# Two tiles instead of three for gathered embedding rows, and the gathers of a time step issued behind the transposes of the step two before it

## The chip, the cores and the metric

The kernel runs on one core of one Trainium2 chip. The metric is the device time of one execution in microseconds. Before the change the median of three runs is 1648.53 us (1646.59 to 1648.6).

## The reference

A batch of 1024 sequences, each of 50 item numbers, is looked up in an embedding table of 100001 rows of 128 numbers. Row 0 counts as zero.

```
emb    = emb_table.at[0].set(0.0)
e      = emb[seq]                                  # 1024 x 50 x 128
prefix = cumsum(e, axis=1)
uF     = prefix / minimum(t_idx, lengths)          # running mean
y      = (uF - mean) * rsqrt(var + 1e-5) * gamma + beta   # mean, var over the batch, per step
step:    v = v + (x - v) / 2; spike = v >= 1; v = v - spike     # 50 steps, one after the other
scores = spikes.mean(axis=0) @ emb.T               # 1024 x 100001
```

The output alone is 409.6 MB. The 50 steps depend on one another through the prefix sum and through v.

## The kernel before, in words

The kernel has two stages. The first works through the 50 time steps and makes the spike counts, a 128 x 1024 tile (embedding dimension on partitions, batch along the free dimension). The second multiplies the counts by the table, 1024 rows of it at a time, and stores the scores; it is bound by those stores and is not touched by the change.

A time step t of the first stage (the loop at L296) goes like this.

- POOL gathers: gather(t) (L192) takes a tile "e" of the pool "gather" (L170) and issues eight indirect DMAs (L195), called lanes here, each of 128 rows of 512 bytes. The tile is 128 x 1024 numbers.
- PE: eight transposes of the gathered tile (L308), four for each half of the batch, accumulate onto the prefix sum in the two PSUM banks "pre". Two further matmuls, correct(t+1) (L268), one for each half, prepare the next step: they take off the rows that items with number 0 have put in. They are issued after the transposes of step t but each waits for DVE to have read its half of "pre".
- DVE: for each half, L317 makes the running mean uF out of "pre", and L318 its statistics. Then come L322, a few small operations, the resting potential (L284), the spike count (L287) and the new v (L345). Every fifth step, only() (L258) makes the weights of the next five corrections.
- ACT: the square root (L326), the centring of uF (L327), the scaling into v (L342), and the comparison with the threshold (L280).

In steps 42 and 44, prepare() transposes and splits a first block of the table for the second stage (L358 to L370; its eight transposes are at L123).

The order of each engine's instructions is the order in which the program issues them (a manual schedule); waits are put between engines where a tile is written, read or used again. A pool with bufs=n hands out n tiles in turn: a new tile of the same tag waits until the last use of the tile n before it has ended. So with three tiles, lane 0 of gather(t+2), issued at the head of step t (L299), waits for the last transposes of step t-1. On POOL's queue there is nothing else during the loop; all later gathers stand behind a lane that waits. Each lane also waits for the same lane of the gather before to have landed (eight completion semaphores, used in turn), and each transpose waits for the landing of its own lane.

Ahead of the loop two tiles of the same pool serve the setup: isz (a 0/1 mask of the items with number 0) and rb (the reciprocal lengths), L203 and L204; each is transposed by PE (L212, L231) and then free. gather(0) is issued behind their allocation, gather(1) just ahead of the loop (L295). The uF tiles come from another pool with two tiles (L169), of the same size. After the loop one output tile of the second stage's first products is taken from the pool "gather" as well (L397).

Of the kernel before, what the change touches and what calls it, by code (L numbers as in the profile page):

```python
# [12 lines left out]
F32 = mybir.dt.float32  # L13
# [7 lines left out]
P = 128  # L21
# [15 lines left out]
def rec_kernel(  # L37
# [10 lines left out]
    B, T = seq.shape  # L48
    N, D = table.shape
    NB = B // P  # L50
# [30 lines left out]
    def pair(i):  # L81
        free.append([embp.tile([P, HALF], F32R, tag=f"{x}{i}", name=f"{x}_{i}") for x in ("hi", "lo")])
# [54 lines left out]
    def prepare(q, pt):  # L137
        turned(q, pt)
        split[q] = hi, lo = free.pop(0)
        hw = size(q)  # L140
        if hw % 2:
            nc.vector.memset(hi[:, hw : hw + 1].bitcast(F32), 0.0)
            nc.vector.memset(lo[:, hw : hw + 1].bitcast(F32), 0.0)
        vp, vh, vl = views(q, pt, hi, lo)
        nc.scalar.copy(vh, vp)  # L145
        nc.vector.tensor_tensor(vl, vp, vh.bitcast(F32), ALU.subtract)  # L146
# [18 lines left out]
    with ExitStack() as ph:  # L165
# [1 line left out]
        lp = ph.enter_context(tc.tile_pool(name="lif", bufs=1))  # L167
        sp = ph.enter_context(tc.tile_pool(name="stats", bufs=3))
        up = ph.enter_context(tc.tile_pool(name="uF", bufs=2))  # L169
        gp = ph.enter_context(tc.tile_pool(name="gather", bufs=3))  # L170
        accp = ph.enter_context(tc.tile_pool(name="acc", bufs=1, space=bass.MemoryType.PSUM))
        vp = ph.enter_context(tc.tile_pool(name="v", bufs=1, space=bass.MemoryType.PSUM))

# [18 lines left out]
        def gather(t):  # L192
            es[t] = gp.tile([P, B], F32, tag="e", name=f"e_{t}")
            for n in range(NB):
                nc.gpsimd.indirect_dma_start(  # L195
                    out=es[t][:, n * P : (n + 1) * P],
                    out_offset=None,
                    in_=table,
                    in_offset=bass.IndirectOffsetOnAxis(ap=idx[:, n, t : t + 1].bitcast(U32), axis=0),
                )  # L200

        make_identity(nc, ident)
        isz = gp.tile([P, NB, P], F32, tag="e", name="isz")  # L203
        rb = gp.tile([P, NB, P], F32, tag="e", name="rb")  # L204
        gather(0)

        nc.vector.memset(isz, 0.0)
# [45 lines left out]
        def only(t):  # L253

            k = t % ONLY
            if k == 0:
                n = min(ONLY, T - t)
                nc.vector.tensor_tensor(  # L258
                    ls[:, :n, :],
                    r0n.unsqueeze(1).to_broadcast([P, n, D]),  # L260
                    sel[:, t : t + n].unsqueeze(2).to_broadcast([P, n, D]),
                    ALU.mult,
                )
            return ls[:, k, :]

        def correct(t, l):
            for h in range(B // BANK):
                nc.tensor.matmul(  # L268
                    pre[h],
                    lhsT=l,  # L270
                    rhs=zT[:, h * BANK : (h + 1) * BANK],
                    start=t == 0,
                    stop=False,
                    skip_group_check=True,
                )

        def over(t, v):

            d = lp.tile([P, B], BF16, tag="d", name=f"d_{t}")
            nc.scalar.activation(d, v, AF.Identity, bias=less)  # L280
            return d

        def rest(d, v):
            nc.vector.scalar_tensor_tensor(negv, d, 0.0, v, ALU.is_ge, ALU.subtract)  # L284

        def spiked(out, cs, v):
            nc.vector.scalar_tensor_tensor(out, v, V_TH, count[:, cs], ALU.is_ge, ALU.add)  # L287
# [7 lines left out]
        gather(1)  # L295
        for t in range(T):  # L296
            last = t == T - 1
            if t + 2 < T:
                gather(t + 2)  # L299
            e = es.pop(t)  # L300
            if last:
                rest(d, v)
                spiked(count, whole, v)
            uF = up.tile([P, B], F32, tag="uF", name=f"uF_{t}")
            bs = sp.tile([P, B // BANK, 6], F32, tag="bs", name=f"bs_{t}")
            for h, cs in enumerate(halves):
                for k in range(0, BANK, P):
                    nc.tensor.matmul(  # L308
                        pre[h][:, k : k + P],
                        lhsT=e[:, h * BANK + k : h * BANK + k + P],  # L310
                        rhs=ident,
                        start=False,
                        stop=last,
                        is_transpose=True,
                        skip_group_check=True,
                    )
                nc.vector.scalar_tensor_tensor(uF[:, cs], rlen[:, cs], 1.0 / (t + 1), pre[h], ALU.max, ALU.mult)  # L317
                nc.vector.bn_stats(bs[:, h, :], uF[:, cs])  # L318
            if not last:
                correct(t + 1, l)  # L320
            mv = sp.tile([P, 2], F32, tag="mv", name=f"mv_{t}")
            nc.vector.bn_aggr(mv, bs.rearrange("p h s -> p (h s)"))  # L322


            r = sp.tile([P, 1], F32, tag="r", name=f"r_{t}")
            nc.scalar.activation(r, mv[:, 1:2], AF.Sqrt, bias=eps)  # L326
            nc.scalar.activation(uF, uF, AF.Identity, bias=mv[:, 0:1], scale=-1.0)  # L327


            if t and not last:  # L330
                rest(d, v)

            nc.vector.reciprocal(r, r)
            q = sp.tile([P, 1], F32, tag="q", name=f"q_{t}")
            nc.vector.scalar_tensor_tensor(q, mv[:, 1:2], BN_EPS, r, ALU.add, ALU.mult)
            nc.vector.tensor_scalar(q, q, r, 3.0, ALU.mult, ALU.subtract)
            a = sp.tile([P, 1], F32, tag="a", name=f"a_{t}")
            nc.vector.tensor_scalar(a, q, r, hgb[:, 0:1], ALU.mult, ALU.mult)  # L338


            def x(vt, cs):
                nc.scalar.activation(vt, uF[:, cs], AF.Identity, bias=hgb[:, 1:2], scale=a)  # L342

            def step(vt, cs):
                nc.vector.scalar_tensor_tensor(vt, negv[:, cs], -0.5, vt, ALU.mult, ALU.add)  # L345

            if not last:
                vt = vp.tile([P, B], F32, tag=f"v{t % 2}", name=f"v_{t}")
                x(vt, whole)
                if t:  # L350
                    spiked(count, whole, v)
                step(vt, whole)
                v = vt
                d = over(t, v)
                if t + 2 < T:
                    l = only(t + 2)

                if t in (T - 8, T - 6):  # L358
                    q = (t - T + 8) // 2
                    pair(q)  # L360
                    prepare(q, vp.tile([P, HALF], F32, tag="v1", name=f"pt_{q}"))
                    if q == TWICE - 1:
                        for k in range(TWICE):
                            rows[GROUP + k] = first[:, k, :]
                        nc.sync.dma_start(
                            out=first[:, :TWICE, :],
                            in_=table[GROUP * HALF : (GROUP + TWICE) * HALF, :].rearrange(
                                "(q p k) d -> p q (k d)", p=P, k=KQ
                            ),
                        )  # L370
# [54 lines left out]
    for c, W in enumerate(WIDTHS):  # L425
# [30 lines left out]
        for n in range(NB):  # L456
            if c == 0 and n == 0:
                continue
            pool, tag, most = turns[blocks % len(turns)]
# [51 lines left out]
```

## Time and profile before

| | |
|---|---|
| median of three runs | 1648.53 us |
| the profiled execution, its own time | 1649.66 us |
| its span in the profile | 1647.8 us |
| mean granted PE clock | 0.791 |
| busy over the span: PE, DVE, ACT, POOL | 65%, 57%, 41%, 23% |
| first stage, 0 to 580 us: PE, DVE, ACT, POOL busy | 177.1, 361.2, 184.8, 381.4 us |
| first stage: granted PE clock, DMA share | 0.52, 0.26 |
| second stage, 580 to 1647.8 us: PE, DVE, ACT, POOL busy | 892.6, 582.8, 484.4, 0.0 us |
| second stage: granted PE clock, DMA share | 0.94, 0.98 |

The page of the profile cuts the span into 40 slices and prints the busy share of each engine in tenths; lists the costliest groups of instructions by line, with count, total and mean time, and the idle time ahead of them with what ended most of it; and follows the chain of work that ended last. Other views list waits by engine and line, instructions in order of time, and busy times by stretch. In a timeline each line has the start in us, the duration, the engine, the line of the program, the operation, output and inputs, and in brackets the idle time of the engine ahead of it and what ended it. A releaser called "remote" or "issue" is one that the profile could not name. An instruction on POOL that issues an indirect DMA is recorded as busy while the descriptors are made; the transfer comes after.

In the text a gather, a step or a transpose is counted from 0 by its order in the trace, which is the order of the program: gather(t) is the eight lanes of step t.

### The profile page before, as it was taken

The page shows a single profiled execution, that of the slowest core. Times are in us where ns is not written, and L with a number is a line of the kernel's source. Part 1 is how long each engine was busy: PE and PEld are TensorE (multiplying, and loading weights), DVE is VectorE, ACT ScalarE, POOL GpSimd, SP SyncE. Part 2 cuts the span into 40 slices and gives each one's busy share as a digit, 9 for nine tenths or more (in the row PEclk, how much of TensorE's full clock was granted, in tenths as well). Part 3 has the DMA queues.
Part 4 walks back from the last instruction along what each step waited for, and adds up shares of the span by engine and source line. Part 5 has one row for each costly group of instructions (what it writes and reads, how often), then busy time and mean ns, then how long its engine had stood idle before and what let it go on. Part 6 is the DMA issues. An engine that isn't in the chain of part 4 may idle for free.

```text
span 1647.8 us, 12231 instructions
## 1 busy us (share of the span) xinstructions
PE 1069.7 (65%) x4450; PEld 816.8 (50%) x4450; DVE 944.0 (57%) x1122; ACT 669.2 (41%) x697; POOL 381.4 (23%) x406
## 2 busy tenths in 40 slices
PE   4233332222322488888988888888887888888884
PEld 2022221111211376666866666666666666666763
DVE  5366665656665866556755455555555555555552
ACT  2133332323322455455644444444444444444442
POOL 7676666666666500000000000000000000000000
PEclk7555555555555589999999999989999999999998
DMA  9511111111111269999999999999999999999998
GB/s 345 209 50 46 46 47 46 45 46 49 46 45 46 64 285 416 405 421 418 399 425 429 430 429 423 416 434 418 427 427 416 416 421 417 428 427 423 396 431 342
DMA packets 53689, 488.12 MB, mean 296 GB/s; under 512 B 11995, under 2 KB 12796, under 8 KB 32380
## 3 DMA queue, kind: packets, MB, share of 16 engines
q1 hardware_dynamic: 32256, 429.81, 62.0%
q0 software_dynamic: 12800, 26.24, 5.9%
q10 hardware_dynamic: 8572, 31.28, 4.8%
q8 instruction: 35, 0.57, 0.1%
q14 instruction: 26, 0.21, 0.0%
HBM read 77.69 MB, written 409.60 MB: 296 GB/s over the span
## 4 chain that ended last, share of the span: by engine, by line
DMA 45%; DVE 20%; PE 11%; another core or an unknown queue 10%; ACT 7%; issue 4%; POOL 1%; ACTq 0%; SPq 0%; DVEq 0%
DMA scores<-o 45%; PE po L153 10%; ACT o L471 5%; DVE bs L318 4%; DVE uF L317 3%; DVE v L345 3%; DVE negv L284 3%; DVE count L287 2%; ACT v L342 2%; DVE o L469 1%; POOL e L195 1%; PE pre L268 1%; DVE a L338 1%; DVE mv L322 1%
## 5 line engine op out<-in xcount | busy, mean ns | idle before, releaser
L469 DVE TENSOR_SCALAR o<-po 128x1024 f32<-128x1024 f32 x391 | 464.4, 1221 | 344.7 <-DMA scores<-o 310.4
L471 ACT ACTIVATE o<-po 128x1024 f32<-128x1024 f32 (+1 forms) x391 | 389.7, 1018 | 538.8 <-DMA scores<-o 324.6
L195 POOL DMA_INDIRECT e<-in_L_rec_emb_table,idx x400 | 380.7, 952 | 184.6 <-issue 114.9
L153 PE MATMUL po<-pairs,countB 128*128 128x512 f32 x1136 | 305.1, 414 | 59.8 <-ACT o L471 42.8
L268 PE MATMUL pre<-zT,ls 128*128 128x512 f32 x100 | 78.7, 789 | 364.1 <-DVE uF L317 267.1
L153 PEld LDWEIGHTS po<-pairs,countB 128*128 128x128 f32 x1136 | 218.0, 197 | 122.9 <-ACT o L471 57.9
L153 PE MATMUL po<-pairs,countC 128*128 128x512 f32 x852 | 236.4, 424 | 44.8 <-ACT o L471 44.8
L268 PEld LDWEIGHTS pre<-zT,ls 128*128 128x128 f32 x100 | 28.8, 289 | 407.7 <-DVE uF L317 297.2
L153 PEld LDWEIGHTS po<-pairs,countC 128*128 128x128 f32 x852 | 167.0, 203 | 90.7 <-ACT o L471 56.3
L317 DVE SCALAR_TENSOR_TENSOR uF<-rlen,pre 128x512 f32<-128x512 f32 x100 | 68.0, 680 | 168.1 <-remote 101.2
L146 DVE TENSOR_TENSOR pairs<-pt,pairs 128x1024 fp32r<-128x1024 f32 x71 | 86.3, 1222 | 93.3 <-ACT pairs L145 93.2
L326 ACT ACTIVATE r<-mv,eps 128x1 f32<-128x1 f32 x50 | 14.7, 295 | 283.2 <-DVE mv L322 179.5
L123 PE MATMUL pt<-ident,rows 128*128 128x128 f32 x782 | 113.8, 294 | 8.7 <-issue 4.9
L123 PEld LDWEIGHTS pt<-ident,rows 128*128 128x128 f32 x782 | 103.5, 155 | 27.5 <-issue 13.2
L308 PE MATMUL pre<-ident,e 128*128 128x128 f32 x400 | 101.0, 422 | 16.1 <-DMA e<-in_L_rec_emb_table,idx 14.9
L153 PE MATMUL po<-hi,countB 128*128 128x512 f32 x216 | 89.1, 412 | 19.4 <-ACT o L471 16.8
L308 PEld LDWEIGHTS pre<-ident,e 128*128 128x128 f32 x400 | 83.6, 221 | 31.6 <-DMA e<-in_L_rec_emb_table,idx 21.8
L153 PE MATMUL po<-lo,countB 128*128 128x512 f32 x216 | 86.7, 403 | 0.0
L280 ACT ACTIVATE d<-v,less 128x1024 bf16<-128x1024 f32 x49 | 54.5, 1113 | 63.6 <-DVE v L345 45.4
L153 PE MATMUL po<-hi,countC 128*128 128x512 f32 (+1 forms) x162 | 68.4, 422 | 15.7 <-ACT o L471 15.7
L145 ACT CAST pairs<-pt 128x1024 fp32r<-128x1024 f32 x71 | 71.8, 1012 | 15.4 <-PE pt L123 15.2
L153 PE MATMUL po<-pairs,countA 128*128 128x512 f32 x284 | 71.3, 394 | 8.2 <-ACT o L471 8.1
(67 smaller groups left out, 844.5 us busy)
## 6 DMA issues: line engine op xcount, KB each, us to landing
scores<-o SPq DMA_DIRECT2D x96, 3072.0 KB
scores<-o SPq DMA_DIRECT2D x32, 1536.0 KB
scores<-o SPq DMA_DIRECT2D x30, 1024.0 KB
rows<-in_L_rec_emb_table ACTq DMA_DIRECT2D x19, 1536.0 KB
scores<-o SPq DMA_DIRECT2D x8, 2896.5 KB
rows<-in_L_rec_emb_table SPq DMA_DIRECT2D x6, 3072.0 KB
e<-in_L_rec_emb_table,idx POOLq DMA_INDIRECT x400
rows<-in_L_rec_emb_table SPq DMA_DIRECT2D x1, 1024.0 KB
```

The lines of the kernel that those rows point to most:

```text
L123: nc.tensor.transpose(pt[:, k0 : k0 + kw], r[:kw, k0 : k0 + D], ident[:kw, :kw])
L145: nc.scalar.copy(vh, vp)
L146: nc.vector.tensor_tensor(vl, vp, vh.bitcast(F32), ALU.subtract)
L153: nc.tensor.matmul(po[:, :kw], lhsT=counts[n], rhs=part[:, k0 : k0 + kw], start=j == 0, stop=j == 1,)
L195: nc.gpsimd.indirect_dma_start(out=es[t][:, n * P : (n + 1) * P], out_offset=None, in_=table, in_offset=bass.IndirectOffsetOnAxis(ap=idx[: ...
L268: nc.tensor.matmul(pre[h], lhsT=l, rhs=zT[:, h * BANK : (h + 1) * BANK], start=t == 0, stop=False, skip_group_check=True,)
L280: nc.scalar.activation(d, v, AF.Identity, bias=less)
L308: nc.tensor.matmul(pre[h][:, k : k + P], lhsT=e[:, h * BANK + k : h * BANK + k + P], rhs=ident, start=False, stop=last, is_transpose=True, ...
L317: nc.vector.scalar_tensor_tensor(uF[:, cs], rlen[:, cs], 1.0 / (t + 1), pre[h], ALU.max, ALU.mult)
L318: nc.vector.bn_stats(bs[:, h, :], uF[:, cs])
L469: nc.vector.tensor_scalar_mul(o[:, h0 : h0 + hw], po[:, :hw], 1.0 / T)
L471: nc.scalar.mul(o[:, h0 : h0 + hw], po[:, :hw], 1.0 / T)
```

## The change

The pool "gather" gets two tiles in place of three. The setup tiles isz and rb are taken from the uF pool (which has two tiles) and no longer from "gather". In the loop the call gather(t + 2) stands behind the transposes of step t and the operations on uF, and no longer at the head of the step. Lane 0 of gather(t+2) then waits for the last transpose of step t, whose tile it fills again. The number and kind of all instructions stay as they were, as does the order on PE, DVE, ACT, POOL and SP.

```diff
-        gp = ph.enter_context(tc.tile_pool(name="gather", bufs=3))
+        gp = ph.enter_context(tc.tile_pool(name="gather", bufs=2))
...
-        isz = gp.tile([P, NB, P], F32, tag="e", name="isz")
-        rb = gp.tile([P, NB, P], F32, tag="e", name="rb")
+        isz = up.tile([P, NB, P], F32, tag="uF", name="isz")
+        rb = up.tile([P, NB, P], F32, tag="uF", name="rb")
         gather(0)
...
         gather(1)
         for t in range(T):
             last = t == T - 1
-            if t + 2 < T:
-                gather(t + 2)
             e = es.pop(t)
...
                 nc.vector.bn_stats(bs[:, h, :], uF[:, cs])
+            if t + 2 < T:
+                gather(t + 2)
             if not last:
                 correct(t + 1, l)
```

## The prediction

> **What bounds the kernel now.** I read the page first: slices, then groups.
>
> ```profile
> span 1647.8 us, 12231 instructions
> ...
> POOL 7676666666666500000000000000000000000000
> PEclk7555555555555589999999999989999999999998
> DMA  9511111111111269999999999999999999999998
> ...
> L195 POOL DMA_INDIRECT e<-in_L_rec_emb_table,idx x400 | 380.7, 952 | 184.6 <-issue 114.9
> ...
> L317 DVE SCALAR_TENSOR_TENSOR uF<-rlen,pre 128x512 f32<-128x512 f32 x100 | 68.0, 680 | 168.1 <-remote 101.2
> ```
>
> There are two stages. Up to about 580 us the 50 time steps run: DMA nearly idle, PE at half clock, POOL in every slice. After that the score stores keep the DMA engines at 0.98 (windows view, 580 to the end). The change touches the first stage; the second should start earlier or later by whatever the first gains or loses. POOL issues 400 gathers; a start-to-start of 1.2485 us (0.944 busy, 0.30 issue) makes 9.99 us a step. DVE's L317 waits 168 us. What POOL waits for, in the waits view:
>
> ```profile
> POOL e L195 <- issue: 114.9, 377, 0.3
> POOL e L195 <- remote: 55.5, 10, 7.8
> POOL e L195 <- PE pre L268: 8.5, 2, 5.4
> ```
>
> Twelve waits of 3.0 to 7.8 us, 60.4 us in all above the usual 0.30. The timelines of POOL, DVE and PE show where (start, duration, idle before):
>
> ```profile
> 302.88 0.94 POOL L195 DMA_INDIRECT e<-in_L_rec_emb_table,idx  x1 [0.30 <-issue]
> 309.13 0.94 POOL L195 DMA_INDIRECT e<-in_L_rec_emb_table,idx  x1 [5.30 <-remote]
> ...
> 354.28 0.94 POOL L195 DMA_INDIRECT e<-in_L_rec_emb_table,idx  x1 [5.51 <-remote]
> ```
>
> ```profile
> 303.95 0.69 DVE L317 SCALAR_TENSOR_TENSOR uF<-rlen,pre 128x512 f32<-128x512 f32 x1 [9.68 <-issue]
> ...
> 308.89 0.69 DVE L317 SCALAR_TENSOR_TENSOR uF<-rlen,pre 128x512 f32<-128x512 f32 x1 [3.53 <-remote]
> ...
> 314.94 0.68 DVE L317 SCALAR_TENSOR_TENSOR uF<-rlen,pre 128x512 f32<-128x512 f32 x1
> ...
> 322.34 0.68 DVE L317 SCALAR_TENSOR_TENSOR uF<-rlen,pre 128x512 f32<-128x512 f32 x1
> ```
>
> ```profile
> 310.23 1.91 PE L308 MATMUL pre<-ident,e 128*128 128x128 f32 x8
> ...
> 333.64 1.91 PE L308 MATMUL pre<-ident,e 128*128 128x128 f32 x8
> 349.85 0.80 PE L268 MATMUL pre<-zT,ls 128*128 128x512 f32 x1 [14.30 <-DVE uF L317]
> ```
>
> Counting instructions by step: steps 25, 26, 27 take 7.4, 7.4 and 8.7 us, then one step takes 21.7; the round repeats every 45.15 us. In the long step (28) the gathers landed by 330.0 us and the transposes are recorded at 333.6 to 335.6, yet L317 starts at 349.11 and 354.05. The trace's record of PE's semaphore gives why: in the short steps it rises every 0.21 us, in the long one every 2.1 to 2.8 us. I call this a **late spell**. Each begins 12 to 23 us after POOL resumed. It ends 4.5 to 5.3 us after POOL stopped (10 of 12 cases; 2.7 and 7.5 in the other two), the intervals shrinking 2.8, 1.4, 0.7, then none. POOL stops because lane 0 of a gather waits until its tile's last transposes are reported. So a round is 32 gathers x 1.2485 = 39.95, plus a stop of 5.2. What makes PE's reports late the profile doesn't say. A count fits them: about 20 reports on credit, refilled one per 2.7 us while POOL gathers and wholly by 5 us of POOL silence. A step has 10 reports (8 transposes, 2 corrections). At 30 us after a resume 20 + 30/2.7 = 31 reports are covered and 29 needed; at 40 us 35 are covered and 39 needed. Hence four steps per round.
>
> **What the Trainium skill says.** "Perfetto Trace Analysis", section "DMA Instruction — SWDGE (GPSIMD)": the recorded end of such a DMA is the end of descriptor making, not of the transfer. The trace agrees: data packets start 0.7 us after the 0.944 us record ends, and the last semaphore write is 1.2 to 1.3 us after it (4.0 in the first 50 us, beside the row loads). "DMA: Bandwidth & Descriptors", section "Anatomy of one DMA — SWDGE (gpsimd) path": a semaphore wait is held on the issuing sequencer, the DMA engines don't wait. It agrees: while lane 0 waits, nothing moves (12 GB/s at 303.83 to 309.13). "TensorE: Matmul & The Clock Gate", section "Seeing it yourself", warns that clock records can be wrong and tells of a quarter clock. The record here stays at 0.50 through late and prompt steps alike; a quarter clock would turn 0.21 us into 0.42 (my estimate from that page), not 2.8, so I don't explain the spells by it.
>
> **The change part by part.** No instruction is added or removed; work per engine stays.
> - isz and rb move to the uF pool. gather(1) and gather(2) lose their waits for those tiles; POOL never stopped there (issue gaps of 0.30 from 3.96 to 75.51). Worth 0. uF_0 and uF_1 now wait for the setup transposes, over by 12 us, ahead of when L317 needs the tiles at 17.85 and 25.3. Cost 0.
> - The eight gathers of step t+2 move in program order from ahead of step t's transposes to behind them. They are the only work on POOL's queue, and no SP or ACT DMA is moved past. A place in the program costs POOL nothing; only the wait does.
> - The wait: lane 0 of gather(t+2) now waits for step t's last transpose, where it waited for step t-1's. Seven gathers are queued behind it on POOL, then the next step's eight; PE's transposes of t+2 wait for them.
>
> Between late spells this wait is free: when POOL comes to gather(t+2), 10 us have passed since gather(t+1) began, and step t's report came about 2 us after gather(t)'s end. Within a round let R be the resume, on the report of step t. Now: step t+1 was gathered, reports at R+3 (as 309.13 to 312.1); t+2 at R+12 and t+3 at R+22, paced by the landings (8 x 1.25 + 1.3 + 0.6). Before they came at R+10.4 and R+23.2. Credit allows the 29th report at about R+23, so t+3 is in before R+30, when gather(t+5) needs it: no stop. Step t+4 isn't in by R+40: stop, 5.2 us. Again four steps and 45.15 us. The lost lead of one tile is covered because both versions hold 40 reports between two stops; if that cover goes, each further stop costs 5.1.
>
> Now the ends. First stop: before gather(7), at 75.51 (step 4 reported at 83.0). After: before gather(5), at 55.14; three transposes of step 3 outstanding, resume about 60.2. Ten rounds: gather(45) at 60.2 + 451.5 = 511.7. The two prepare calls (steps 42, 44) add 8 transposes each, which in the run before shortened the last round to two steps; I take three: 45, 46, 47 to 541.7, stop to 546.9, gathers 48 and 49 to 566.9. The run before ended its gathers at 566.57 after 12 stops; here 12 stops too. POOL gains nothing.
>
> The gain is in the tail. Before, gather(48) resumed at 546.91 with step 45 reported, and four steps of DVE's chain remained: last L317 at 579.25, 12.7 us after the last gather. After, the same resume comes with step 46 reported: L317 of step 47 at +5.8 = 552.7, of 48 at +7.4 = 560.1, of 49 at +10.9 = 571.0 (567.46 to 579.25 was 11.8, 0.9 of it a late report). Gather(49) lands at 568.2, its reports by 569 to 572. So 571 to 572, **7.5 us earlier**; if the last stop falls before gather(49), 557.1 + 16.7 = 573.8, 5.5 earlier. I take 6.5. Against the profiled execution's own 1649.66 (span 1647.8 and 1.9 around it) that is 1643.2; it lay 1.1 above the median 1648.53, so the forecast is **1642.0**. Last unknown, the first stop: if silence ends before credit is full (as at 394.19, 4.6 us, whose next spell came after 12 us), one more stop follows, +5. Own range of this case: 1638 to 1649.
>
> **Rivals.**
> 1. *Shorter rounds: slower.* Place: lane 0 of gather(t+5) at R+30. If step t+3 is reported later than R+30 (margin 7 us, under three late reports), POOL stops there; a stop cut short leaves credit unfilled, and the next spell comes sooner. With three steps a round: 45 steps give 15 stops, 15 x 5.1 + 5.0 = 81 against 60.4, +21, less 6 in the tail: 1663. With two steps a round 22 stops: 1699. For it: the 34.7 us rounds before (gathers 35 to 37) and one tile less of slack. Against: the margin. Chance 0.32, a part of it with only two or three such rounds (1652 to 1660).
> 2. *No late spells.* If regular landings spread PE's reports and credit never ends, POOL runs 3.96 + 502 = 506 and step 49 follows by 511, 68 us earlier: 1580. Against: steps 0 to 2, paced by landings, ended in a spell at 42 us just the same. Chance 0.05.
> 3. *Spells on a timer, or the tail hidden.* 45.15 us recurs closely; if POOL doesn't rule it, the phase of the last spell sets the tail: 1645 to 1651. Against: the rounds of 34 and 23 us, both ended by POOL's silence. Chance 0.15.
> The main case has 0.48.
>
> **Numbers.** 0.2% is 3.3 us, about what a measurement tells from no change: faster is under 1645.2, slower over 1651.8. Main case: 0.42 faster, 0.06 same; rival 1: 0.32 slower; rival 2: 0.05 faster; rival 3: 0.02 faster, 0.13 same. Range 1634 to 1667: it leaves out rival 2, two-step rounds and the ends.
>
> **What would show it.** Right: POOL's first stop near 55 us, then stops of about 5 us every 32 gathers, 12 in all; L317 steps of 10 us in place of 7.4 between spells; last L317 about 5 us behind the last gather; second stage unchanged at about 1067 us. Wrong: over 13 stops, or stops of 1 to 3 us in pairs (rival 1); none (rival 2); long steps that go on with POOL silent (rival 3).

## The result, and the profile after

The changed kernel takes 1640.23 us (median of seven runs, 1637.92 to 1643.46). The kernel before, measured with it, takes 1648.53 (seven runs, 1646.59 to 1654.22). The ratio is 0.9945 with an interval of 0.993 to 0.996: faster by 0.55%, 8.3 us in the medians. The profiled execution took 1643.46, its span is 1641.7 us; that is 6.2 and 6.1 less than in the trace that the prediction argued from.

The page of the changed kernel; L315 here is the line that was L317 before (the transposes are L306 in place of L308):

```profile
span 1641.7 us, 12230 instructions
...
POOL 7666766666665500000000000000000000000000
PEclk9999999999999999999999999999999999999998
DMA  9511111111112189999999999999999999999998
...
L195 POOL DMA_INDIRECT e<-in_L_rec_emb_table,idx x400 | 380.7, 952 | 181.6 <-issue 114.6
...
L315 DVE SCALAR_TENSOR_TENSOR uF<-rlen,pre 128x512 f32<-128x512 f32 x100 | 67.9, 679 | 168.2 <-remote 132.8
```

The busy times of POOL (380.7) and of the running mean (67.9) are those of before, and so is DVE's idle time ahead of it (168.2). POOL's idle time is 3.0 us less (181.6 against 184.6). The clock row reads 9 in the first stage, where it read 5. That is not where the time came from: no clock record of this execution stands before 583 us, and other runs of the same kernel with a mean clock of 0.795 and 0.798 took 1640.48 and 1637.95 us.

What POOL waits for, in the waits view (total us, count, longest):

```profile
POOL e L195 <- issue: 114.6, 371, 1.6
POOL e L195 <- remote: 52.5, 15, 5.5
POOL e L195 <- PE pre L268: 8.4, 2, 4.9
```

More stops, and shorter ones: 18 of over 1 us, where there had been 12, but 57.3 us in all above the usual 0.30, where there had been 60.4. POOL's timeline (start, duration, and in brackets the idle time ahead) shows two forms of them:

```profile
58.55 0.94 POOL L195 DMA_INDIRECT e<-in_L_rec_emb_table,idx  x1 [3.33 <-remote]
71.98 0.94 POOL L195 DMA_INDIRECT e<-in_L_rec_emb_table,idx  x1 [3.50 <-remote]
117.17 0.94 POOL L195 DMA_INDIRECT e<-in_L_rec_emb_table,idx  x1 [5.53 <-remote]
...
217.09 0.94 POOL L195 DMA_INDIRECT e<-in_L_rec_emb_table,idx  x1 [3.68 <-remote]
228.34 0.94 POOL L195 DMA_INDIRECT e<-in_L_rec_emb_table,idx  x1 [1.58 <-remote]
240.30 0.94 POOL L195 DMA_INDIRECT e<-in_L_rec_emb_table,idx  x1 [2.02 <-remote]
274.87 0.94 POOL L195 DMA_INDIRECT e<-in_L_rec_emb_table,idx  x1 [4.91 <-PE pre L268]
...
533.92 0.94 POOL L195 DMA_INDIRECT e<-in_L_rec_emb_table,idx  x1 [2.81 <-remote]
```

The first stop begins at 55.2 (58.55 less 3.33). Some rounds are as before (274.87 to 319.12 is 44.25). Elsewhere (217 to 240) POOL stops three times in a row, ahead of each step, for 1.3 to 3.4 us. DVE's timeline at that place shows what happens:

```profile
216.85 0.69 DVE L315 SCALAR_TENSOR_TENSOR uF<-rlen,pre 128x512 f32<-128x512 f32 x1 [9.07 <-remote]
222.89 0.68 DVE L315 SCALAR_TENSOR_TENSOR uF<-rlen,pre 128x512 f32<-128x512 f32 x1
228.11 0.69 DVE L315 SCALAR_TENSOR_TENSOR uF<-rlen,pre 128x512 f32<-128x512 f32 x1 [3.81 <-remote]
234.88 0.68 DVE L315 SCALAR_TENSOR_TENSOR uF<-rlen,pre 128x512 f32<-128x512 f32 x1
240.06 0.69 DVE L315 SCALAR_TENSOR_TENSOR uF<-rlen,pre 128x512 f32<-128x512 f32 x1 [3.77 <-remote]
```

The first line is the second half of step 17. In steps 18 and 19 the first half of the batch is prompt (222.89, 234.88) and the second half is late by 3.8 us (228.11, 240.06). POOL resumes 0.23 to 0.24 us after each late start (216.85, 228.11, 240.06): both wait for the same report of PE.

The end of the first stage. DVE's timeline of the kernel before, then of the changed one, the running means of steps 48 (two halves) and 49:

```profile
567.46 0.68 DVE L317 SCALAR_TENSOR_TENSOR uF<-rlen,pre 128x512 f32<-128x512 f32 x1
...
569.66 0.69 DVE L317 SCALAR_TENSOR_TENSOR uF<-rlen,pre 128x512 f32<-128x512 f32 x1 [0.80 <-PE pre L268]
...
579.25 0.68 DVE L317 SCALAR_TENSOR_TENSOR uF<-rlen,pre 128x512 f32<-128x512 f32 x1
```

```profile
554.94 0.68 DVE L315 SCALAR_TENSOR_TENSOR uF<-rlen,pre 128x512 f32<-128x512 f32 x1
...
561.95 0.69 DVE L315 SCALAR_TENSOR_TENSOR uF<-rlen,pre 128x512 f32<-128x512 f32 x1 [5.60 <-remote]
...
571.54 0.68 DVE L315 SCALAR_TENSOR_TENSOR uF<-rlen,pre 128x512 f32<-128x512 f32 x1
```

From the second half of step 48 to step 49 it is 9.59 us in both (569.66 to 579.25, 561.95 to 571.54): the chain through v. So the start of that second half sets the end of the stage. It comes 7.71 us earlier, and so does step 49. POOL's last resume and its last lane before, then the last lane after the change (its last resume is the line at 533.92 above):

```profile
546.91 0.94 POOL L195 DMA_INDIRECT e<-in_L_rec_emb_table,idx  x1 [3.03 <-PE pre L268]
...
565.63 0.94 POOL L195 DMA_INDIRECT e<-in_L_rec_emb_table,idx  x1 [0.30 <-issue]
```

```profile
562.64 0.94 POOL L195 DMA_INDIRECT e<-in_L_rec_emb_table,idx  x1 [0.30 <-issue]
```

The last gather ended at 563.58, where it had ended at 566.57. Of the 7.7 us, 3.0 are thus POOL's and 4.7 the distance from the last gather to step 49 (I call it the **tail**: 12.7 us before, 8.0 after). The second stage took 1070.2 us from step 49 to the end of the span, before 1068.6; over all traces in which late spells occur it is 1067.8 to 1070.2, so 1.6 us of difference is scatter.

### The profile page after: what moved, and what is told of

It is laid out like the page before. It is cut to its first block, busy times and chain, and to the rows that moved or that the text cites. A ratio compares the mean times of both kernels' runs of the same rounds, so it can differ in the third digit from the quotient of the medians.

```text
span 1641.7 us, 12230 instructions
## 1 busy us (share of the span) xinstructions
PE 1088.2 (66%) x4450; PEld 809.8 (49%) x4450; DVE 943.2 (57%) x1122; ACT 668.2 (41%) x697; POOL 381.4 (23%) x406
## 4 chain that ended last, share of the span: by engine, by line
DMA 47%; POOL 11%; DVE 11%; PE 10%; another core or an unknown queue 7%; issue 7%; ACT 6%; ACTq 0%; SPq 0%; DVEq 0%; POOLq 0%
DMA scores<-o 46%; POOL e L195 11%; PE po L153 10%; ACT o L471 5%; DVE bs L316 2%; DVE uF L315 2%; DVE v L345 2%; DVE o L469 2%; DVE negv L284 1%; DVE count L287 1%; DMA e<-in_L_rec_emb_table,idx 1%; ACT v L342 1%; DVE a L338 0%; DVE mv L322 0%
## 5 line engine op out<-in xcount | busy, mean ns | idle before, releaser
L195 POOL DMA_INDIRECT e<-in_L_rec_emb_table,idx x400 | 380.7, 952 | 181.6 <-issue 114.6
L153 PEld LDWEIGHTS po<-pairs,countB 128*128 128x128 f32 x1136 | 217.5, 197 | 124.5 <-ACT o L471 61.7
L153 PE MATMUL po<-pairs,countC 128*128 128x512 f32 x852 | 232.8, 419 | 49.0 <-ACT o L471 48.9
L268 PE MATMUL pre<-zT,ls 128*128 128x512 f32 x100 | 78.9, 791 | 275.1 <-DVE uF L315 225.5
L268 PEld LDWEIGHTS pre<-zT,ls 128*128 128x128 f32 x100 | 29.3, 294 | 314.7 <-DVE uF L315 253.9
L306 PE MATMUL pre<-ident,e 128*128 128x128 f32 x400 | 124.5, 435 | 75.5 <-DMA e<-in_L_rec_emb_table,idx 56.9
L315 DVE SCALAR_TENSOR_TENSOR uF<-rlen,pre 128x512 f32<-128x512 f32 x100 | 67.9, 679 | 168.2 <-remote 132.8
L306 PEld LDWEIGHTS pre<-ident,e 128*128 128x128 f32 x400 | 80.6, 209 | 120.5 <-DMA e<-in_L_rec_emb_table,idx 86.4
L123 PE MATMUL pt<-ident,rows 128*128 128x128 f32 x782 | 111.1, 289 | 9.3 <-issue 4.9
L123 PEld LDWEIGHTS pt<-ident,rows 128*128 128x128 f32 x782 | 100.8, 152 | 27.8 <-issue 12.9
```

The source lines that it names most:

```text
L123: nc.tensor.transpose(pt[:, k0 : k0 + kw], r[:kw, k0 : k0 + D], ident[:kw, :kw])
L153: nc.tensor.matmul(po[:, :kw], lhsT=counts[n], rhs=part[:, k0 : k0 + kw], start=j == 0, stop=j == 1,)
L195: nc.gpsimd.indirect_dma_start(out=es[t][:, n * P : (n + 1) * P], out_offset=None, in_=table, in_offset=bass.IndirectOffsetOnAxis(ap=idx[: ...
L268: nc.tensor.matmul(pre[h], lhsT=l, rhs=zT[:, h * BANK : (h + 1) * BANK], start=t == 0, stop=False, skip_group_check=True,)
L306: nc.tensor.matmul(pre[h][:, k : k + P], lhsT=e[:, h * BANK + k : h * BANK + k + P], rhs=ident, start=False, stop=last, is_transpose=True, ...
```

## The experiments

Two theories stood against each other. **T** (called A in the first texts below): the tiles of the last steps make the gain, since with two tiles less of the chain is left when POOL's last gather ends. **B**: the body of the stage makes it, by another rhythm of stops. Rival P gives the gain to the place of the gathers or to the setup tiles. To these come the prediction's credit of PE reports as the cause of the spells (also called A, with C as its rival), and a theory **D** that the gathers delay PE's reports, by POOL's making of the descriptors (narrow form) or by their landings (wide form). All times are compared within one set of runs on one chip, because of what the first set showed.

### First set: four kernels, and no late spells at all

Three tiles again, all else as changed (setup tiles in the uF pool, gathers behind the transposes):

```diff
-        gp = ph.enter_context(tc.tile_pool(name="gather", bufs=2))
+        gp = ph.enter_context(tc.tile_pool(name="gather", bufs=3))
```

> The changed kernel with three gather tiles again; the gathers stay behind the transposes, the setup tiles stay in the uF pool. Theory A (the two tiles, through the position of POOL's last stops against the chain of the last steps, made the gain; place and setup tiles cost nothing): the time of the kernel before, 1648 to 1651 us, last L315 near 579 us, about 12 stops of 5 us. Rival P (the place of the gathers or the setup tiles made the gain): 1639 to 1643 us.

Three tiles up to step 39 and two from step 40 on, by tags of their own; and the reverse. Of the diffs only the lines that differ are shown; in both kernels `slot` is a dictionary made ahead of `gather`, the pool has bufs=1 for each tag, and the output tile after the loop takes the tag "e0":

```diff
-            es[t] = gp.tile([P, B], F32, tag="e", name=f"e_{t}")
+            back = 3 if t < 40 else 2
+            slot[t] = slot[t - back] if t >= back else t
+            es[t] = gp.tile([P, B], F32, tag=f"e{slot[t]}", name=f"e_{t}")
```

```diff
-            es[t] = gp.tile([P, B], F32, tag="e", name=f"e_{t}")
+            back = 2 if t < 40 else 3
+            slot[t] = 2 if t == 40 else slot[t - back] if t >= back else t
+            es[t] = gp.tile([P, B], F32, tag=f"e{slot[t]}", name=f"e_{t}")
```

> The changed kernel with three gather tiles in turn up to step 39 and two from step 40 on. Theory A (the gain sits in the tail: POOL's last resume is released by a step one later, so that fewer steps of the chain remain behind the last gather): 1639 to 1643 us, last L315 5 to 8 us behind the last gather. Rival B (two tiles shorten the sum of POOL's stops in the body of the loop): 1646 to 1649 us.

> The changed kernel with two gather tiles up to step 39 and three from step 40 on. Theory A (tail): 1646 to 1650 us, last L315 about 12 us behind the last gather. Rival B (body): 1640 to 1643 us.

One small matmul for each half takes the waits for the four landings, so that PE reports 2 times in most steps (4 times in every fifth) where it had reported 10 times; it now has 12 matmuls a step, of which two are added:

```diff
+        junk = accp.tile([P, HALF], F32, tag="po0", name="junk")
...
             for h, cs in enumerate(halves):
+                if h in (0, 1):
+                    nc.tensor.matmul(junk[:1, :4], lhsT=ident[:, :1], rhs=e[:, h * BANK : (h + 1) * BANK : P], start=True, stop=True)
                 for k in range(0, BANK, P):
```

> The changed kernel with one added matmul of 1 x 4 per half of a step, which reads a column of each of the four gathered lanes and so takes their landing waits; the four transposes behind it then have no wait of their own and report to the semaphore once together. PE's reports fall from 10 to 2 a step; its waits, its transposes and POOL's work stay. Theory A (late spells come from the number of reports that PE makes while POOL gathers, about 20 on credit and one more per 2.7 us): no spell, no stop of POOL, last gather ends near 510 us, last L315 at 511 to 518, 1580 to 1588 us. Rival C (spells come by PE's clock, a timer or POOL's running time, whatever PE reports): spells and stops as now, 1637 to 1645 us.

Measured: the kernel before took 1578.11 us here (49 runs, 1576.59 to 1579.71), 70 us less than where it was first measured. The three kernels with other tiles took 1577.83, 1578.36 and 1577.91: ratios 1.0001 [0.9992, 1.0009], 1.0003 [0.9995, 1.0011] and 1.0001 [0.9993, 1.0009]. The one with fewer waits took 1579.33, 1.0011 [1.0004, 1.0018]. What had been expected with late spells was not tested, since none occurred. The page and the waits of the three-tile kernel:

```profile
span 1575.8 us, 12229 instructions
...
POOL 7777777777776000000000000000000000000000
```

```profile
POOL e L195 <- issue: 117.3, 385, 0.3
POOL e L195 <- DMA e<-in_L_rec_emb_table,idx: 3.4, 11, 0.3
POOL e L195 <- DMA idx<-in_r_seq: 2.7, 1, 2.7
POOL e L195 <- PE pre L306: 0.9, 3, 0.3
```

No wait ahead of a gather is over 0.3 us, but for the first one, which waits for the indices. POOL gathers without a pause, its digit is 7 in place of 6, the last gather ends at 505.34 and step 49's running mean starts at 507.00. That is rival 2's state (its sum was 506 and 1580), and by its time (1578.11) the kernel before is in it as well. It teaches two things: the late spells cost some 70 us of 1648, and where they don't occur the tiles count for nothing, because all that PE and DVE do hides behind 400 x 1.2485 us of gathering. The changed kernel itself wasn't run in such a set; four kernels that differ from it in one edit each were.

### Second set: the changed kernel again

> The changed kernel as it is, beside the kernel before. In the four runs ahead of this one both had no late spell at all (1578 us). Theory A (the change can gain or lose only where POOL is stopped by late reports; without them lane 0's wait is always met): ratio 1.000 within 0.001 if there are no spells, 0.993 to 0.996 if there are. Rival P (a gain in itself, by the place of the gathers or the setup tiles): 0.995 with or without spells.

Unchanged code, a set in which spells occur: 1643.42 us against 1651.04, ratio 0.9953 [0.9938, 0.9969]. The gain repeats. After two shorter rounds at the start, and with some shorter ones later on, its POOL timeline has the rounds that the prediction had worked out:

```profile
106.09 0.94 POOL L195 DMA_INDIRECT e<-in_L_rec_emb_table,idx  x1 [5.00 <-PE pre L268]
151.22 0.94 POOL L195 DMA_INDIRECT e<-in_L_rec_emb_table,idx  x1 [5.32 <-remote]
196.37 0.94 POOL L195 DMA_INDIRECT e<-in_L_rec_emb_table,idx  x1 [5.48 <-remote]
241.58 0.94 POOL L195 DMA_INDIRECT e<-in_L_rec_emb_table,idx  x1 [5.57 <-PE pre L268]
286.73 0.94 POOL L195 DMA_INDIRECT e<-in_L_rec_emb_table,idx  x1 [5.52 <-remote]
```

They are 45.13, 45.15, 45.21 and 45.15 us apart, with two tiles. So the triple short stops of the first trace aren't a property of two tiles; the same program makes one form or the other.

### Third set: three tiles, and fewer reports, where spells occur

The two kernels are those of the first set, with their edits shown there.

> The changed kernel with three gather tiles again, sent once more because the first time no late spell came in any kernel. Where there are spells, theory A (the two tiles make the gain, through the position of POOL's last stops): ratio to the kernel before 0.999 to 1.001. Rival P (place of the gathers, setup tiles): 0.993 to 0.996. Without spells both say 1.000.

> The kernel with one small matmul per half that takes the landing waits, so that PE reports 2 times a step in place of 10, sent once more for the same reason. Where there are spells, theory A (spells come from the number of PE's reports while POOL gathers): no stop of POOL, last gather ends near 506 us, last L315 near 511, 1578 to 1586 us, as where there are no spells. Rival C (spells whatever PE reports): 1637 to 1645 us. Without spells both say 1578 to 1580.

Three tiles: 1648.43 us against 1648.65, ratio 0.9993 [0.9982, 1.0003]. The gain is gone, so the place of the gathers in the program and the setup tiles bring nothing, and the number of tiles brings all of it. POOL still had 17 stops, with triples of short ones among them (92.7, 104.7), and ended at 564.16, about where the changed kernel's POOL ends. What came back is the tail, 11.8 us. Its last stop in POOL's timeline, and DVE's steps 48 and 49:

```profile
544.49 0.94 POOL L195 DMA_INDIRECT e<-in_L_rec_emb_table,idx  x1 [3.44 <-remote]
```

```profile
565.05 0.68 DVE L315 SCALAR_TENSOR_TENSOR uF<-rlen,pre 128x512 f32<-128x512 f32 x1
...
566.37 0.67 DVE L315 SCALAR_TENSOR_TENSOR uF<-rlen,pre 128x512 f32<-128x512 f32 x1
...
575.94 0.68 DVE L315 SCALAR_TENSOR_TENSOR uF<-rlen,pre 128x512 f32<-128x512 f32 x1
```

None of these waits for anything but the chain: steps 46, 47 and 48 start at 550.29, 557.70 and 565.05, 7.4 us apart, from the resume at 544.49 on. That is the tail of the kernel before once more.

Fewer reports: 1649.92 us, ratio 1.0005 [0.9993, 1.0016], with two tiles. Its waits, and DVE's steps 48 and 49 (L319 here):

```profile
POOL e L195 <- issue: 109.3, 358, 0.6
POOL e L195 <- remote: 57.9, 16, 4.3
POOL e L195 <- PE pre L268: 3.7, 1, 3.7
```

```profile
559.63 0.69 DVE L319 SCALAR_TENSOR_TENSOR uF<-rlen,pre 128x512 f32<-128x512 f32 x1 [3.75 <-remote]
568.72 0.69 DVE L319 SCALAR_TENSOR_TENSOR uF<-rlen,pre 128x512 f32<-128x512 f32 x1 [7.67 <-remote]
578.30 0.68 DVE L319 SCALAR_TENSOR_TENSOR uF<-rlen,pre 128x512 f32<-128x512 f32 x1
```

With 2 reports a step in place of 10 the spells don't become rarer. Most rounds are three steps long (32.4 to 34.1 us), the stops last 1.5 to 4.0 us above the usual 0.30, and POOL is silent for 58.3 us in all. A credit that each report draws on is refuted. A count of PE's instructions, of which this kernel has two more a step, was not tried. The kernel also shows a limit of T: the last spell fell on step 48, whose second half started at 568.72, 3.8 us after POOL had ended, and with that the gain of two tiles was lost.

### Fourth set: less gathering, and other loads

Six of the eight lanes are gathered, and the transposes of the other two read the first lane of their half again:

```diff
-            for n in range(NB):
+            for n in (0, 1, 2, 4, 5, 6):
...
-                        lhsT=e[:, h * BANK + k : h * BANK + k + P],
+                        lhsT=e[:, h * BANK + k % (3 * P) : h * BANK + k % (3 * P) + P],
```

> The changed kernel with six of the eight lanes gathered in each step; the two others are left out and their transposes read the first lane of their half once more, so the sums are of other rows; PE's 8 transposes, 2 corrections and 10 reports a step stay. Where there are spells: theory D (each gather leaves a debt that only POOL's silence pays: the five runs with spells had 57.3 to 60.4 us of silence for 400 gathers, whatever the number of tiles or of PE's reports, about 0.146 us a gather): 300 gathers, 40 to 48 us of silence, last gather ends at 420 to 428, 1492 to 1505 us. Theory A (credit of about 20 PE reports, one more per 2.7 us of POOL's running): 10 reports against 2.8 in the 7.5 us of a step, rounds of under three steps, 80 us of silence or more, last gather ends beyond 455, 1530 us or more. Without spells: last gather ends at 381, 1455 us.

Plain loads of neighbouring table rows from SP, in place of the gathers:

```diff
-                nc.gpsimd.indirect_dma_start(
-                    out=es[t][:, n * P : (n + 1) * P],
-                    out_offset=None,
-                    in_=table,
-                    in_offset=bass.IndirectOffsetOnAxis(ap=idx[:, n, t : t + 1].bitcast(U32), axis=0),
-                )
+                c0 = (t * NB + n) * P
+                nc.sync.dma_start(out=es[t][:, n * P : (n + 1) * P], in_=table[c0 : c0 + P, :])
```

> The changed kernel with each gather of 128 rows replaced by a plain load of 128 neighbouring rows from SP's queue: the lookup is left out, bytes, lanes, landing semaphores, PE's transposes and reports stay, and POOL does nothing in the loop. The loads stand behind the first row loads, so the loop starts near 57 us. Where there are spells: theory D in its narrow form (the debt comes from the descriptors that POOL makes): no late report, steps of 7.4 us by DVE's chain, last L315 near 440 to 450, 1508 to 1522 us. Theory D in its wide form (the debt comes with each landing, 16 semaphore writes a lane, whoever issues it): steps of 11 us on the mean, last L315 near 620, 1690 us. Without spells: as the narrow form.

No spells in this set either (the kernel before took 1578.41). Six lanes took 1467.38, ratio 0.9295 [0.9268, 0.9322]; plain loads 1501.98, 0.9514 [0.9487, 0.9542]. About the spells they say nothing. Without spells, though, they show what bounds the stage: with six lanes the last gather ends at 384.67, 120.7 us before the 505.34 of eight lanes, where two lanes of 50 steps at 1.2485 us come to 124.9. With plain loads most steps take 7.35 us (every fifth 8.09), DVE's own chain. The kernel with six lanes keeps PE's ten matmuls a step but not their ten reports: in most steps its trace has 2, one for each half, which its expectation had not foreseen.

Six lanes show one more thing. POOL stops just twice for over 1 us, ahead of gather(45) (1.57 us) and of gather(47), and that without a spell. The second stop, and PE's queue at that place:

```profile
362.52 0.94 POOL L195 DMA_INDIRECT e<-in_L_rec_emb_table,idx  x1 [3.75 <-PE pre L306]
```

```profile
358.60 1.94 PE L123 MATMUL pt<-ident,rows 128*128 128x128 f32 x8 [3.32 <-DVE count L287]
360.33 1.91 PE L306 MATMUL pre<-ident,e 128*128 128x128 f32 x8
```

Gather(47) waits for the transposes of step 45 (L306). They stand on PE's queue behind those of prepare() in step 44 (L123), and PE idles ahead of L123 for 3.3 us, which the profile puts down to DVE's spike count. Gather(45) waits in the same way for step 43, behind the prepare() of step 42. In the traces with spells the same 3.31 us stand ahead of L123 in step 44, with two tiles and with three.

The later sets brought the second kernel of the first set twice more, and the plain loads once.

> Three gather tiles up to step 39, two from step 40 on, sent once more because the first time there were no late spells. Where there are spells: theory T (POOL's silence is about 58 us with two tiles and with three, so POOL ends at the same time; the gain is that fewer steps of the chain remain behind the last gather, which the tiles of the last steps alone decide): 1639 to 1643 us, ratio 0.993 to 0.997, last L315 6 to 9 us behind the last gather. Rival B (two tiles in the body of the loop make the gain): 1647 to 1650 us, ratio 0.999 to 1.001, 12 us behind. Without spells both say 1578.

Again no spells: 1577.68 us, 0.9999 [0.9991, 1.0007] of the kernel before.

> Each gather replaced by a plain load of 128 neighbouring rows from SP's queue (the lookup is left out), sent once more because the first time there were no late spells; there it took 1502 us with steps of 7.4 us. Where there are spells: theory D in its narrow form (the debt comes from POOL making descriptors): no late report, 1495 to 1512 us. In its wide form (the debt comes with each landing of 128 rows, whoever issues it, at about 1.39 us a lane): steps of 11 us on the mean, 1660 to 1700 us. Rival C (spells by PE's clock or a timer): one step of 20 us in four, 1650 us or more.

No spells: 1502.49 us against 1577.98, 0.9522 [0.9494, 0.955]. So D, in its narrow and its wide form, was never put to the test and stays open.

### Two tiles from step 40 on, where spells occur

The third run of that kernel met spells; it is the one that tells T from B.

> Three gather tiles up to step 39, two from step 40 on, a third time, since twice no late spell came. Where there are spells: theory T (the tiles of the last steps make the gain): 1639 to 1643 us, ratio 0.993 to 0.997, last L315 6 to 9 us behind the last gather. Rival B (two tiles in the body make it): 1647 to 1650 us, ratio 0.999 to 1.001, 12 us behind. Without spells both say 1578.

It took 1640.25 us (1636.37 to 1644.7; the traced execution is the slowest, 1644.7) against 1648.47 (1646.92 to 1656.1), ratio 0.9941 [0.992, 0.9962]: the whole gain, with three tiles for the first 40 of 50 steps. POOL didn't gain: it was silent for 61.7 us, with one stop of 9.3 us where the tiles change from three to two, and its last gather ended at 567.95, later than before. The tail is 5.8 us. Its last stop, and DVE's steps 48 and 49 (L318 here, and L198 for the gather):

```profile
538.31 0.94 POOL L198 DMA_INDIRECT e<-in_L_rec_emb_table,idx  x1 [4.04 <-remote]
```

```profile
559.99 0.68 DVE L318 SCALAR_TENSOR_TENSOR uF<-rlen,pre 128x512 f32<-128x512 f32 x1
...
564.13 0.69 DVE L318 SCALAR_TENSOR_TENSOR uF<-rlen,pre 128x512 f32<-128x512 f32 x1 [2.73 <-remote]
...
573.77 0.68 DVE L318 SCALAR_TENSOR_TENSOR uF<-rlen,pre 128x512 f32<-128x512 f32 x1
```

B falls, by this run; the reverse kernel, with two tiles up to step 39 and three at the end, never ran where spells occur. The traces with spells side by side (one execution each; silence is POOL's idle time ahead of gathers above 0.30):

| kernel | stops over 1 us | silence | last resume | last gather ends | step 48, second half | step 49 | tail |
|---|---|---|---|---|---|---|---|
| before (three tiles) | 12 | 60.4 | 546.91, gather(48) | 566.57 | 569.66 | 579.25 | 12.7 |
| three tiles again | 17 | 57.9 | 544.49, gather(48) | 564.16 | 566.37 | 575.94 | 11.8 |
| changed (two tiles) | 18 | 57.3 | 533.92, gather(47) | 563.58 | 561.95 | 571.54 | 8.0 |
| changed, again | 14 | 59.4 | 535.35, gather(47) | 565.00 | 562.20 | 571.78 | 6.8 |
| two tiles from step 40 | 12 | 61.7 | 538.31, gather(47) | 567.95 | 564.13 | 573.77 | 5.8 |
| two tiles, fewer reports | 18 | 58.3 | 535.23, gather(47) | 564.90 | 568.72 | 578.30 | 13.4 |

In each of them the last resume is the report of step 45. The wait ahead of L123 that the six lanes showed is a likely reason, since it holds up this step's transposes in every kernel. The stop ahead of the last one fits it too: in five of the six it is for step 43, behind the other prepare() (gather(45) with two tiles, gather(46) with three; only with two tiles from step 40 on is it gather(44)). No run moves prepare(), so this is argued and not shown. With two tiles it is gather(47) that waits for this report, with three gather(48), and so POOL's last pause lies a step earlier in the gathering: at 533.9 to 538.3, not at 544.5 to 546.9. From there DVE has four steps to go either way. The columns on the right show the step that follows: step 49 is 9.57 to 9.64 us behind the second half of step 48 in all six.

## Why the prediction was right, and where its working was not

**The result.** Forecast 1642.0, a gain of 6.5 us; measured 1640.23, a gain of 8.3. The mechanism named for it, a shorter tail because POOL is one tile less ahead at its last pause, is shown by the runs: three tiles take the gain away (0.9993), two tiles in the last ten steps alone bring all of it (0.9941). The way it comes about was foreseen in part only. The prediction kept the last resume where it was, at 546.9 ahead of gather(48), and had step 46 release it, so that one step less of DVE's chain remained. In the traces step 45 still releases it and four steps remain; it is gather(47) that resumes, 9.8 us earlier on the mean (533.92, 535.35, 538.31 against 546.91, 544.49), about one gather of 9.99. From there to step 49 it takes 35.5 to 37.6 us where it had taken 31.5 to 32.3, so 4.6 us of the 9.8 are lost again and 5.2 remain (step 49 at 571.54, 571.78, 573.77 against 579.25, 575.94). This is all that these executions differ by: their spans are 5.1 us apart on the mean. The medians of the same five runs are 7.2 us apart on the mean; two of the three traces with two tiles are the slowest executions of their run (1643.46, 1644.7), so the other 2 us are a matter of which executions were traced.

**The parts costed at nothing** (setup tiles, place in the program) were nothing: 0.9993 [0.9982, 1.0003] with both as in the changed kernel and three tiles.

**First stop.** Expected at 55.14 with a resume at 60.2; measured 55.2 and 58.55. The silence was shorter than expected and a second stop followed 13 us later (71.98). The prediction had that as its last unknown, at +5 us. The second stop came and the +5 did not.

**Twelve stops of 5.2 us, in rounds of four steps.** This step failed in its form. There were 18 stops, and triples of 1.3 to 3.4 us, which the prediction had put down as the sign that it was wrong. The second trace of the same kernel has the rounds almost as worked out, and three tiles give 17 stops on one chip and 12 on another: the form isn't governed by the number of tiles. What holds is the sum. The prediction priced a further stop at 5.1 us because it took each one to be of full length; in the six traces 12 to 18 stops come to 57.3 to 61.7 us, 0.14 to 0.15 us for each of 400 gathers. A stop cut short is followed by a sooner one, as rival 1 said, but the sum over all stops stays. That is why rival 1's 1663 did not come, though its stops did. (In the trace before, ten of the stops reached their report after 4.3 to 5.5 us, not 4.5 to 5.3; nothing hangs on it.)

**POOL gains nothing, gathers end at 566.9.** They ended at 563.58, 3.3 us sooner, but also at 564.16 with three tiles and at 567.96 with two at the end: the change doesn't set it.

**The tail of 4.1 us** (566.9 to 571.0) was 8.0. The prediction let DVE's chain run free from its last resume, to step 48 at 560.1 and step 49 at 571.0. In the trace the last resume lay 13 us earlier, with three gathers of POOL behind it in place of two, and a further spell came in that time: it made the second half of step 48 start at 561.95, after 5.6 us of waiting, and step 49 follows that half. (The same half waited 4.4 us in the second trace of this kernel and 2.7 with two tiles from step 40 on.) The tail was too short by 3.9 us and the end of gathering too late by 3.3; the two errors nearly cancel, and the last L315 at 571.5 hits the 571 to 572 partly by luck. In the kernel with fewer reports the same kind of spell came later and cost the whole gain: so much of rival 3, the phase of the last spell, is true.

**Steps of 10 us between spells** were expected in place of 7.4. They are still 7.4 (for example 274.63 to 282.00 for second halves): between spells the chain catches up as before. Only where short stops follow one another are they 11.3 and 12.0 (216.85 to 228.11 to 240.06).

**The cause of the spells** in the prediction, 20 reports on credit and one more per 2.7 us, is refuted by the kernel with fewer reports. The forecast needed only that a stop of POOL ends with the report that it waits for and that prompt reports follow, which the six traces show. Since POOL stops for just that report, they don't show that the silence itself is what helps. **Rival 2** (1580) was given 0.05 as an effect of the change; it exists, at 1578, for the kernel before and for kernels within one edit of the changed one, and isn't an effect of the change.

## What to carry to other kernels

Here the producer paused for much the same sum over a stage (57.3 to 61.7 us), and fewer buffers didn't raise it; they decided how far the consumer was behind at the last pause, and so what was left when the producer ended. Look at the last pause before pricing buffers by the pauses in between. Ask for each step which one of its two halves the last chain hangs on: here one start time set the end of the stage in every trace with spells. A theory of a count is worth little until a kernel has changed the count, and a stall that one set of runs shows should be looked for in another before kernels are built against it.

## What the runs showed of the hardware that was not expected

- Late spells are not a property of the program. The kernel before takes 1645.5 to 1656.1 us in the runs with spells and 1576.6 to 1579.7 in those without; each set of runs was wholly of one kind. Spells occurred in the first measurement and in three of the seven sets after it. Whether the chip or something else about the set decides isn't known: two sets that bore the same chip number differ. Every execution on record was taken with its span and its granted clock, so the runs don't tell either whether recording has a part in it.
- With spells, POOL is silent for 57.3 to 61.7 us per 400 indirect DMAs of 128 rows; without them it doesn't pause, with the same start-to-start of 1.2485 us. Within a spell the reports of DVE to PE stay prompt: in the trace before, L268 starts at 349.85, 0.05 us after L317 (349.11, for 0.69) has ended. What makes PE's reports late remains open.
- In the traces with spells records of semaphores are missing: before the change 1197 of PE's 1384 are there (without spells 1383 or 1384), and most of all those of the eight semaphores that count the gathers' landings. Each of these has 84 to 276 records with spells and, with eight lanes, 798 to 802 without, in the trace before about 3 in place of 16 for each landing. It may be an effect of the same cause; no run tells. The prediction read its landings (1.2 to 1.3 us after the record of the POOL instruction, 4.0 in the first 50 us) from what was there. With all 16, in the three-tile kernel without spells, the last one mostly comes 1.5 to 1.7 us after it, and 4.5 to 5.5 in the first 50 us; no sum of the prediction turns on the difference.
- PEclk in the first stage reads 5 or 9 without regard to the time: without spells it is 9 in the three-tile kernel and 5 in the one with six lanes, with spells 5 before the change and 9 after. The Trainium skill, "TensorE: Matmul & The Clock Gate", section "Seeing it yourself", warns that these records can be wrong; in the changed kernel's trace the 9 only meant that no record stood before 583 us.
